# Head of a hybrid block: constants, loads and bias spread rearranged, rstd by GpSimd's power, batch 0's routing inside batch 1's scan

## Chip, cores and metric

The kernel runs on 1 core of one Trainium2 chip. The metric is device time in microseconds (us) of a run; less is better. Before the change it is 1699.86 us, the median of 6 runs (1697.03 to 1704.3).

## The reference

The input x is 8 batches of 512 tokens of 256 numbers, all float32. Four residual steps follow one another, each on a layernorm of x (written `_ln` here; mixture is `_L0_ffn_ref`, used twice with the same weights):

```python
x = x + scan(_ln(x))        # xi = silu(x @ Win + bin); h = 0.9*h + xi*Bp over time; y = h.Cp + Dp*xi; y @ Wout + bout
x = x + mixture(_ln(x))     # router, 4 of 16 experts (2 of 4 groups first), plus 2 shared experts
x = x + attention(_ln(x))   # 16 heads of 16, causal, scores clipped to +-10
x = x + mixture(_ln(x))
```

Since the decay is the same for all states, the scan of the 16 states of a channel is one scan of xi, times the sum over j of Bp * Cp. The bias bout is added to each token.

## The kernel before

A batch of 512 tokens is four tiles of 128 tokens (`NT`); features are taken in two halves (`KD`), the 512 scan channels in four columns of 128 (`NI`). There are four stages: the scan of all batches with the first mixture's routing and shared experts beside it (`stretch(Scan())`), the first mixture's routed blocks (`routed(0, ...)`), the attention with the second mixture's routing (`stretch(Attention())`), and the second mixture's routed blocks. The change lies in the first stage, which ends at about 370 us.

**Order.** Each engine runs its instructions in order; a planner chooses that order when the program is built, from the order in which the program issues them and from its own estimate of their times. `keep_in_program_order` pins an instruction, `issue_after` puts one behind another on the same engine. The program issues in pieces: `Piece` is a count of TensorE columns and a generator of steps; `behind` joins pieces one after another, `beside` interleaves them so that each has done the same share of its columns, and `timed` places the steps of a piece at given shares of what it is beside (0.2 is a fifth of the way). One pass of the loop at L1439 is called a slot here: slot b holds batch b's scan, batch b - 1's routing, batch b - 2's shared experts, and the norm and transposes of batch b + 1.

**Head.** `load_x(0)` brings batch 0's x (L147). GpSimd makes the identity (L173) and issues the DMAs of small weights (L180 to L197); bout goes through a DMA that spreads it over 128 partitions (L190). Then GpSimd makes the constants: `before` (L234), `causal` (L272), `tri` (L279), `ones` (L284), `region` by 16 memsets (L290), `steps`, `number`, `zeros` (L322). ACT issues the load of the scan's Win (L178) and Wout (L188).

**A norm** (`normed`, L436): VectorE takes statistics of each tile (L443, L444), and then rstd, the root's reciprocal, in one of two ways: by VectorE, three Newton steps after a start from the bits (L451 to L459), or by one addition on VectorE and a power on GpSimd (L462, L463). Then VectorE writes the normed tiles (L468). Batches 0 and 1 of the scan take the first way, and their instructions are pinned. `turned` (L393) transposes normed tiles on TensorE (L405) and copies them out of PSUM (L407).

**A scan** (`Scan.main`, L523) takes per column two matmuls into pz (L531), a sigmoid on ACT (L540), on VectorE the product (L541), the scan (L543) and, after ACT's scaling by Dp (L544), y (L547). Its steps are: four columns, one step of no work, then the projection by Wout (`add_projection`, 16 matmuls, L485), whose halves VectorE adds to x (L494). `Scan.project` (L514) adds bout to x on GpSimd (L518). Its `Piece` counts 10240 columns.

**Routing.** `Route` (L581): norm of the batch's x into `sorted_m`, transposes, the router's matmuls (`logits`, L622), then `choices` (L652): five steps of picking on VectorE (`PICKS`, L655 to L699), one with counting matmuls by tri and ones (L707, L708), two for slots and gains (the last instruction, L744, is kept in `gained`), and 16 steps, each with one indirect DMA from GpSimd (L758). In the scan stage the normed tiles of a batch are put behind the `gained` of the batch before (L603, L466). `shared_experts` (L1092) has 12 steps: eight of two wide matmuls (L1107), each pair of steps followed by ACT and VectorE (L1125 to L1127), and four of the down projection (L1136).

**The first two batches** (`first_two`, L1416): batch 0 is normed and turned before it. It issues load 2, batch 1's norm, the products of Bp and Cp (two entries of `pending`), batch 0's four columns, batch 1's transposes, bias sums and four columns, and batch 0's projection. What is left of batch 1's scan goes into slot 1, beside batch 0's routing with its picks, and batch 2's norm and transposes. Slot 2 begins the shared experts (batch 0's), and holds the rest of batch 0's choices.

Of the kernel before, what the change touches and what calls it, by code (L numbers as in the profile page):

```python
# [35 lines left out]
BLK = P  # L36
# [29 lines left out]
BY_PE = 3  # L66

# [15 lines left out]
def tile_hybrid_block(  # L83
# [87 lines left out]
    load_x(0)  # L171
    ident = const.tile([P, P], FP, name="ident")
    make_identity(nc, ident)  # L173

# [3 lines left out]
    nc.scalar.dma_start(out=w_in_sb, in_=w_in.rearrange("(p k) i -> p k i", p=P))  # L178
    b_in_sb = const.tile([P, NI], FP, name="b_in_sb")
# [14 lines left out]
    nc.gpsimd.memset(rw_sb, 0.0)  # L194
    nc.gpsimd.dma_start(out=rw_sb[:, :, 0:E], in_=router_t.rearrange("(p k) e -> p k e", p=P))
    rb_sb = const.tile([P, E], FP, name="rb_sb")
    nc.gpsimd.dma_start(out=rb_sb, in_=route_bias.partition_broadcast(P))  # L197
# [24 lines left out]
    def load_expert(e: int):  # L222
# [11 lines left out]
    nc.gpsimd.memset(before, 1.0)  # L234
    nc.gpsimd.affine_select(
        out=before,
        in_=before,
        compare_op=ALU.is_gt,
        fill=0.0,
        base=0,  # L240
        pattern=[[1, EG], [-1, EG]],
        channel_multiplier=0,
    )
    neg_half = const.tile([P, NT], FP, name="neg_half")
    nc.gpsimd.memset(neg_half, -0.5)
# [11 lines left out]
    def load_attention_weights():  # L257
# [14 lines left out]
    nc.gpsimd.memset(causal, TOP)  # L272
    nc.gpsimd.affine_select(
        out=causal, in_=causal, compare_op=ALU.is_ge, fill=0.0, base=0, pattern=[[0, 2], [1, P]], channel_multiplier=-1
    )
# [3 lines left out]
    nc.gpsimd.memset(tri, 1.0)  # L279
    nc.gpsimd.affine_select(  # L280
        out=tri, in_=tri, compare_op=ALU.is_gt, fill=0.0, base=0, pattern=[[1, P]], channel_multiplier=-1
    )
    ones = const.tile([P, P], FP, name="ones")
    nc.gpsimd.memset(ones, 1.0)  # L284
# [4 lines left out]
    for e in range(E):  # L289
        nc.gpsimd.memset(region[:, e : e + 1], float(e * REG))  # L290
    steps = const.tile([P, NJ], FP, name="steps")
    nc.gpsimd.iota(steps, [[BLK, NJ]], base=0, channel_multiplier=0, allow_small_or_imprecise_dtypes=True)
# [29 lines left out]
    nc.gpsimd.memset(zeros, 0.0)  # L322
    nc.gpsimd.iota(zeros[:, D + 2 * TK :].bitcast(I32), [[0, SAME]], base=NTOK, channel_multiplier=1)
# [62 lines left out]
    def issue(piece):  # L386
        for _ in piece.steps:
            pass


# [45 lines left out]
    def normed(b: int, tag: str, place, by_vector: bool = False, pinned: bool = False, past=lambda: None):  # L436
# [24 lines left out]
        else:  # L461
            nc.vector.tensor_scalar(rstd, mv[:, :, 1], EPS, None, ALU.add)  # L462
            nc.gpsimd.tensor_tensor(rstd, rstd, neg_half, ALU.pow)  # L463
# [911 lines left out]
    def stretch(layer):  # L1375
# [60 lines left out]
        begun = None  # L1436
        if layer.mixture == 0:
            begun = first_two()
        for b in range(1 if begun else 0, B):  # L1439
            pieces = [begun or layer.main(b, made.pop(b))]  # L1440
            begun = None
            nxt, last = b + layer.ahead, b == B - 1
            fill = []
            if layer.ahead > 1 and not last:
                fill.append(project(b + 1))
            if b > 1:
                shared_sum = experts(b - 2)
# [8 lines left out]
                pieces.append(timed(sends.pop(), 0.1, 0.14, 0.18, *spread(0.22, 0.66 if last else 0.86, NT * TK)))  # L1456
            if fill:
                pieces.append(behind(*fill))
            if b > 0:
# [3 lines left out]
                else:  # L1463
                    first, then, rows, full = layer.norms
# [8 lines left out]
                else:  # L1473
                    pieces += [
                        timed(r.scores(i == 1), *layer.scores[:2], *spread(*layer.scores[2:], NT)),
                        timed(some(r.rest, PICKS), *spread(*layer.choose, PICKS)),
                    ]
            if nxt < B:
                added = layer.load(nxt)
                if added is not None:  # L1480
# [3 lines left out]
                    timed(turn(nxt), *layer.turns),  # L1484
# [130 lines left out]
```

## Time and profile before

| | |
|---|---|
| median of 6 runs | 1699.86 us |
| the profiled execution: its own time | 1703.75 us |
| its span, first to last instruction | 1701.7 us |
| mean granted TensorE clock | 0.971 of full speed |
| busy, share of the span | PE 93%, PEld 68%, DVE 68%, ACT 44%, POOL 45% |
| batch 0's first normed tile (L468) starts | 8.50 us |
| batch 0's pz (L531) | from 11.62 us |
| batch 1's pz | from 29.10 us |
| batch 0's routing: first transposes (L405) | at 50.97 us |
| batch 2's pz, start of slot 2 | at 58.37 us |
| batch 3's pz, start of slot 3 | at 97.03 us |
| batch 4's pz, start of slot 4 | at 134.67 us |

PE is TensorE, PEld its weight loads (they overlap its matmuls), DVE VectorE, ACT ScalarE, POOL GpSimd; SP issues DMAs. A line of the timeline is: start, duration, engine, line, operation, output<-inputs, count, and in brackets the idle time before it with what ended it. A line of waits is: engine, tile and line that waited <- engine, tile and line that it waited for: us in total, times, longest. A float32 matmul appears as two records, so a step of two matmuls of 512 columns is four records.

### The profile page before, as it was taken

The page shows a single profiled execution, that of the slowest core. Times are in us where ns is not written, and L with a number is a line of the kernel's source. Part 1 is how long each engine was busy: PE and PEld are TensorE (multiplying, and loading weights), DVE is VectorE, ACT ScalarE, POOL GpSimd, SP SyncE. Part 2 cuts the span into 40 slices and gives each one's busy share as a digit, 9 for nine tenths or more (in the row PEclk, how much of TensorE's full clock was granted, in tenths as well). Part 3 has the DMA queues.
Part 4 walks back from the last instruction along what each step waited for, and adds up shares of the span by engine and source line. Part 5 has one row for each costly group of instructions (what it writes and reads, how often), then busy time and mean ns, then how long its engine had stood idle before and what let it go on. Part 6 is the DMA issues. An engine that isn't in the chain of part 4 may idle for free.

```text
span 1701.7 us, 34229 instructions
## 1 busy us (share of the span) xinstructions
PE 1585.1 (93%) x9992; PEld 1161.6 (68%) x9992; DVE 1155.6 (68%) x3623; ACT 743.9 (44%) x1461; POOL 758.6 (45%) x655
## 2 busy tenths in 40 slices
PE   6999995969999999999899999999896999999996
PEld 3566663559999999974344444454355999999996
DVE  7988885435677666647877876977753566666664
ACT  3223331125555555555553344353312555555553
POOL 3356654515555555540032422421451555555554
PEclk8999997989999999999999999999998999999998
DMA  4354421527777766641333224231652777777776
GB/s 163 135 197 152 147 97 63 187 61 109 102 126 123 104 99 98 92 73 38 87 95 107 90 88 125 78 104 67 196 182 63 109 102 127 135 135 135 133 135 131
DMA packets 281645, 195.31 MB, mean 115 GB/s; under 512 B 168592, under 2 KB 262064, under 8 KB 281456
## 3 DMA queue, kind: packets, MB, share of 16 engines
q1 hardware_dynamic: 228368, 119.40, 27.5%
q0 software_dynamic: 51984, 72.09, 23.8%
q8 instruction: 85, 1.39, 0.3%
q10 hardware_dynamic: 1104, 1.57, 0.3%
q14 instruction: 104, 0.85, 0.2%
HBM read 89.71 MB, written 103.23 MB: 113 GB/s over the span
## 4 chain that ended last, share of the span: by engine, by line
PE 34%; DVE 10%; DMA 4%; issue 2%; another core or an unknown queue 1%; ACT 1%; POOL 0%; SPq 0%; DVEq 0%; POOLq 0%; ACTq 0%
PE ph L993 13%; PE pyr L1024 6%; PE pd_m L1136 3%; PE pg_m L1107 3%; DMA part<-rows 3%; PE ps_a L1238 2%; PE po_a L1274 2%; DVE w_all L1258 2%; DVE w_all L1259 1%; DMA x<-part 1%; PE py_a L485 1%; PE pv_a L1208 1%; PE pq_a L1190 1%; PE pt L975 1%
## 5 line engine op out<-in xcount | busy, mean ns | idle before, releaser
L1034 POOL DMA_INDIRECT part<-rows x272 | 426.3, 1567 | 340.1 <-ACT rows L1033 252.4
L758 POOL DMA_INDIRECT xg<-sorted_m,slots_m x256 | 259.8, 1015 | 272.9 <-ACT slots_m L755 94.5
L993 PEld LDWEIGHTS ph<-rows,gate 128*128 128x128 f32 x2160 | 277.8, 191 | 33.4 <-ACT rows L976 22.2
L993 PE MATMUL ph<-rows,gate 128*128 128x128 f32 x2160 | 291.5, 278 | 1.9 <-ACT rows L976 1.9
L993 PE MATMUL ph<-rows,up 128*128 128x128 f32 x2160 | 285.3, 275 | 0.0
L1024 PE MATMUL pyr<-w_all,rows 128*128 x1088 | 279.2, 380 | 0.0
L993 PEld LDWEIGHTS ph<-rows,up 128*128 128x128 f32 x2160 | 262.9, 192 | 0.0
L966 DVE COPY up<-w_all 128x512 f32 x270 | 119.1, 442 | 211.4 <-PE ph L993 192.5
L966 ACT COPY gate<-w_all 128x512 f32 x270 | 166.5, 618 | 122.5 <-DVE up L966 55.3
L1024 PEld LDWEIGHTS pyr<-w_all,rows 128*128 128x128 f32 x1088 | 186.9, 192 | 14.3
L1248 ACT ACTIVATE w_all<-ps_a 128x1024 f32<-128x1024 f32 x160 | 155.4, 1021 | 75.7 <-PE ps_a L1238 49.9
L1033 ACT ACTIVATE rows<-pyr,gain 128x256 f32<-128x256 f32 x272 | 128.9, 474 | 80.9 <-PE pyr L1024 60.6
L1001 ACT ACTIVATE rows<-ph 128x256 f32<-128x256 f32 x272 | 104.5, 384 | 114.2 <-PE ph L993 103.0
L1003 DVE TENSOR_TENSOR rows<-ph,rows 128x256 f32<-128x256 f32 x272 | 115.1, 423 | 32.1 <-ACT rows L1001 30.7
L1004 DVE TENSOR_TENSOR rows<-ph,rows 128x256 f32<-128x256 f32 x272 | 115.3, 424 | 26.2 <-issue 0.5
L1136 PE MATMUL pd_m<-sd_sb,act_m 128*128 128x256 f32 x512 | 121.2, 382 | 5.9 <-DVE sig_m L1122 5.7
L1107 PE MATMUL pg_m<-xT_m,su_sb 128*128 128x512 f32 x256 | 125.4, 611 | 0.6 <-issue 0.6
L1107 PE MATMUL pg_m<-xT_m,sg_sb 128*128 128x512 f32 x256 | 123.9, 607 | 0.0
L1238 PE MATMUL ps_a<-w_all 32*128 32x384 f32 (+3 forms) x1024 | 111.4, 478 | 10.9 <-ACT w_all L1248 10.2
L1136 PEld LDWEIGHTS pd_m<-sd_sb,act_m 128*128 128x128 f32 x512 | 95.8, 190 | 27.5 <-DVE sig_m L1122 7.6
L1258 DVE SCALAR_TENSOR_TENSOR w_all<-w_all,causal 128x512 f32<-128x512 f32 (+1 forms) x160 | 92.4, 578 | 28.8 <-ACT w_all L1248 25.5
L1238 PEld LDWEIGHTS ps_a<-w_all 32*128 32x128 f32 x1024 | 48.6, 189 | 72.3 <-ACT w_all L1248 44.7
(213 smaller groups left out, 1960.6 us busy)
## 6 DMA issues: line engine op xcount, KB each, us to landing
rows<-xg SPq DMA_DIRECT2D x720, 32.0 KB
rows<-xg SPq DMA_DIRECT2D x92, 134.0 KB
part<-x SPq DMA_DIRECT2D x16, 512.0 KB
part<-ys_m SPq DMA_DIRECT2D x14, 512.0 KB
sum<-part SPq DMA_DIRECT2D x14, 512.0 KB
w_all<-in_L_ffn_gate_w_dram SPq DMA_DIRECT2D x27, 256.0 KB
w_all<-in_L_ffn_up_w_dram SPq DMA_DIRECT2D x27, 256.0 KB
w_all<-in_L_ffn_down_w_dram SPq DMA_DIRECT2D x27, 256.0 KB
```

Of the source, the lines that this page charges most:

```text
L758: nc.gpsimd.indirect_dma_start(out=xg[i], out_offset=bass.IndirectOffsetOnAxis(ap=slots[:, at : at + 1], axis=0), in_=rows[:, t, :], in_of ...
L966: copy(here, w_all[:, bass.ds(held[n][0] + half * KD * F, KD * F)])
L993: nc.tensor.matmul(ph[s][:, f * P : (f + 1) * P], lhsT=both[s][:, k * F + f * P : k * F + (f + 1) * P], rhs=rows[:, ROW + k * P : ROW + (k ...
L1004: made = nc.vector.tensor_mul(act, ph[1], act)
L1024: nc.tensor.matmul(py, lhsT=act[:, f * P : (f + 1) * P], rhs=w_all[:, bass.ds(w + 2 * KD * F + f * D, D)], start=(f == 0), stop=(f == KF - 1),
L1033: nc.scalar.mul(y, py, gain[:, TK : TK + 1])
L1034: acc = nc.gpsimd.indirect_dma_start(out=parts[i][n % 2], out_offset=bass.IndirectOffsetOnAxis(ap=rows[:, D + 2 * TK : D + 2 * TK + 1].bit ...
L1107: made = nc.tensor.matmul(dst, lhsT=w[:, k, f * P : (f + 1) * P], rhs=xnT[:, k, :], start=(k == 0), stop=(k == KD - 1),)
L1136: nc.tensor.matmul(py[:, j, :], lhsT=acts[n][:, f, t * P : (t + 1) * P], rhs=shared[n][3][:, f, :], start=(n == 0 and f == 0), stop=(n == ...
L1238: nc.tensor.matmul(ps[j // 2][:, j % 2, col : col + n], lhsT=k_sb[w][r, o, c * P : (c + 1) * P], rhs=q_sb[r, o, c * P : T], start=True, st ...
L1248: nc.scalar.activation(es[two], ps[two], AF.Exp, scale=ATT_SCALE)
L1258: nc.vector.scalar_tensor_tensor(diagonal, diagonal, LOW, limit, ALU.max, ALU.min)
```

## The change

It does the following.

- `ones` and `neg_half` are made first, by VectorE; `steps` is dropped; `region` is one iota. `zeros`, the router's loads, `before`, `causal` and `tri` go into a list `late`, which is issued behind the power of batch 1's norm.
- bout is loaded as one row and spread over the partitions by a matmul with a row of ones and a copy on ACT. Wout's load goes from ACT's queue to SP's, behind x 1.
- 14 matmuls of ones by ones (`keep_busy`) stand at TensorE's start, 5 more after batch 0's projection.
- rstd of batches 0 and 1 comes by GpSimd's power; both copies of batch 0's transposes go to ACT.
- In `first_two` the order is: batch 0's bias sums, batch 1's statistics and power, the two products, batch 1's normed tiles, the shared weights' loads, the late constants, load 2; then two columns of batch 0, batch 1's transposes, two columns of batch 0, two of batch 1, batch 0's projection. Two columns of batch 1 and its bias sums are left to slot 1.
- In slot 1 batch 0's routing begins at once (places 0.0 to 0.1), four of the twelve shared-expert steps of batch 0 stand at 0.35 to 0.8, batch 2's transposes at 0.93. The five picks of batch 0 move from slot 1 to the start of slot 2 (0.02 to 0.2), which keeps eight of the expert steps; batch 1's scores and picks move to later places in slot 2.

The diff, cut:

```diff
+IDLE, FIRST, BETWEEN, EARLY = 14, 2, 5, 4
...
     load_x(0)
+    ones = const.tile([P, P], FP, name="ones")
+    nc.vector.memset(ones, 1.0)
+    neg_half = const.tile([P, NT], FP, name="neg_half")
+    nc.vector.memset(neg_half, -0.5)
...
+    b_out_sb = const.tile([P, D], FP, name="b_out_sb")
+    nc.gpsimd.dma_start(out=b_out_sb[0:1, :], in_=b_out.rearrange("(o d) -> o d", o=1))
...
-    nc.scalar.dma_start(out=w_out_sb, in_=w_out.rearrange("(c p) d -> p c d", p=P))
-    b_out_sb = const.tile([P, D], FP, name="b_out_sb")
-    nc.gpsimd.dma_start(out=b_out_sb, in_=b_out.partition_broadcast(P))
     load_x(1)
+    nc.sync.dma_start(out=w_out_sb, in_=w_out.rearrange("(c p) d -> p c d", p=P))
...
-    for e in range(E):
-        nc.gpsimd.memset(region[:, e : e + 1], float(e * REG))
-    steps = const.tile([P, NJ], FP, name="steps")
-    nc.gpsimd.iota(steps, [[BLK, NJ]], base=0, channel_multiplier=0, allow_small_or_imprecise_dtypes=True)
+    nc.gpsimd.iota(region, [[REG, E]], base=0, channel_multiplier=0, allow_small_or_imprecise_dtypes=True)
...
+    def keep_busy(many: int, name: str):
+
+        idle = bank([P, P], f"idle_{name}")
+        for _ in range(many):
+            nc.tensor.matmul(idle, lhsT=ones, rhs=ones, start=True, stop=True)
...
-            nc.vector.tensor_scalar(rstd, mv[:, :, 1], EPS, None, ALU.add)
-            nc.gpsimd.tensor_tensor(rstd, rstd, neg_half, ALU.pow)
+            keep(nc.vector.tensor_scalar(rstd, mv[:, :, 1], EPS, None, ALU.add))
+            powers[tag] = nc.gpsimd.tensor_tensor(rstd, rstd, neg_half, ALU.pow)
+            if pinned:
+                yield
...
-            return normed(b, f"l{i}_{b}", place, first, first)
+            return normed(b, f"l{i}_{b}", place, False, first)
...
+        if i == 0:
+            keep_busy(IDLE, "head")
+            spread_row = bank([P, D], "b_out")
+            nc.tensor.matmul(spread_row, lhsT=ones[0:1, :], rhs=b_out_sb[0:1, :], start=True, stop=True)
+            nc.scalar.copy(b_out_sb, spread_row)
...
-                issue(Piece(0, turn(b, by_both if first else layer.copies)))
-                if first:
-                    load_shared()
-            if b == 0:
+                issue(Piece(0, turn(b)))
+            if b == 0 and i == 1:
                 issue(project(b))
 
         def first_two():
 
-            layer.load(1)
-            issue(Piece(0, norm(1, True)))
+            issue(project(0))
+            second = norm(1, True)
+            issue(Piece(0, some(second, NT + 1)))
             for _ in range(2):
                 pending.pop(0)()
+            issue(Piece(0, second))
+            load_shared()
+            with tc.issue_after(powers["l0_1"].ins):
+                for make in late:
+                    make()
+            layer.load(1)
             main = layer.main(0, made.pop(0))
-            issue(Piece(0, some(main.steps, NI)))
+            issue(Piece(0, some(main.steps, FIRST)))
             issue(Piece(0, turn(1)))
-            issue(project(1))
+            issue(Piece(0, some(main.steps, NI - FIRST)))
+            later_sum = project(1)
             second = layer.main(1, made.pop(1))
-            issue(Piece(0, some(second.steps, NI)))
+            issue(Piece(0, some(second.steps, NI - 2)))
             issue(main)
-            return Piece(second.columns - NI * KD * T, second.steps)
+            keep_busy(BETWEEN, "between")
+            return behind(Piece(second.columns - (NI - 2) * KD * T, second.steps)), later_sum
...
+            scores, choose, turns = layer.scores, layer.choose, layer.turns
+            if i == 0 and b == 1:
+
+                scores, turns = (0.2, 0.22, 0.5, 0.55), (0.93, 0.95)
+            if i == 0 and b == 2:
+                scores, choose = (0.61, 0.65, 0.73, 0.77), (0.79, 0.99)
...
+            if i == 0 and b == 1:
+                piece = experts(0)
+                each = piece.columns // 12
+                started[0] = Piece((12 - EARLY) * each, piece.steps)
+                pieces.append(timed(some(piece.steps, EARLY), *spread(0.35, 0.8, EARLY)))
+                pieces.append(timed(later_sum.steps, *spread(0.12, 0.3, NT)))
             if b > 1:
-                shared_sum = experts(b - 2)
+                shared_sum = started.pop(b - 2, None) or experts(b - 2)
...
+                if i == 0 and b == 2:
+                    pieces.append(timed(sends.pop(), *spread(0.02, 0.2, PICKS), 0.22, 0.24, 0.26, *spread(0.32, 0.88, NT * TK)))
...
-                    first, then, rows, full = layer.norms
+                    first, then, rows, full = layer.norms if i or b > 1 else (0.0, 0.04, 0.06, 0.1)
...
-                        timed(r.scores(i == 1), *layer.scores[:2], *spread(*layer.scores[2:], NT)),
-                        timed(some(r.rest, PICKS), *spread(*layer.choose, PICKS)),
+                        timed(r.scores(i == 1), *scores[:2], *spread(*scores[2:], NT)),
+                        *([timed(some(r.rest, PICKS), *spread(*choose, PICKS))] if i or b > 1 else []),
```

More of the change, by code (lines that the diff above doesn't have):

```diff
@@ L171, in tile_hybrid_block @@
     load_x(0)
+    ones = const.tile([P, P], FP, name="ones")
+    nc.vector.memset(ones, 1.0)
+    neg_half = const.tile([P, NT], FP, name="neg_half")
+    nc.vector.memset(neg_half, -0.5)
     ident = const.tile([P, P], FP, name="ident")
     make_identity(nc, ident)
+    late, powers = [], {}
     w_scan = const.tile([P, 2 * KD * DI], FP, tag="w_sa", name="w_scan")
@@ L187, in tile_hybrid_block, with load_router @@
     w_out_sb = w_scan[:, KD * DI :].rearrange("p (c d) -> p c d", c=NI)
-    nc.scalar.dma_start(out=w_out_sb, in_=w_out.rearrange("(c p) d -> p c d", p=P))
-    b_out_sb = const.tile([P, D], FP, name="b_out_sb")
-    nc.gpsimd.dma_start(out=b_out_sb, in_=b_out.partition_broadcast(P))
     load_x(1)
+    nc.sync.dma_start(out=w_out_sb, in_=w_out.rearrange("(c p) d -> p c d", p=P))
     rw_sb = const.tile([P, KD, SQ], FP, name="rw_sb")
-    nc.gpsimd.memset(rw_sb, 0.0)
-    nc.gpsimd.dma_start(out=rw_sb[:, :, 0:E], in_=router_t.rearrange("(p k) e -> p k e", p=P))
     rb_sb = const.tile([P, E], FP, name="rb_sb")
-    nc.gpsimd.dma_start(out=rb_sb, in_=route_bias.partition_broadcast(P))
+    def load_router():
+        nc.gpsimd.memset(rw_sb, 0.0)
+        nc.gpsimd.dma_start(out=rw_sb[:, :, 0:E], in_=router_t.rearrange("(p k) e -> p k e", p=P))
+        nc.gpsimd.dma_start(out=rb_sb, in_=route_bias.partition_broadcast(P))
+    late.append(load_router)
     pending = []
@@ L233, in tile_hybrid_block, with make_before @@
     before = const.tile([P, EG, EG], FP, name="before")
[L234 to L245, printed above, removed]
+    def make_before():
+        nc.gpsimd.memset(before, 1.0)
+        nc.gpsimd.affine_select(
+            out=before,
+            in_=before,
+            compare_op=ALU.is_gt,
+            fill=0.0,
+            base=0,
+            pattern=[[1, EG], [-1, EG]],
+            channel_multiplier=0,
+        )
+    late.append(make_before)
     decay = const.tile([P, 1], FP, name="decay")
@@ L271, in tile_hybrid_block, with make_causal, make_tri @@
     causal = const.tile([P, 2, P], FP, name="causal")
[L272 to L275, printed above, removed]
-    tri = const.tile([P, P], FP, name="tri")
[L279 to L284, printed above, removed]
+    def make_causal():
+        nc.gpsimd.memset(causal, TOP)
+        nc.gpsimd.affine_select(
+            out=causal, in_=causal, compare_op=ALU.is_ge, fill=0.0, base=0, pattern=[[0, 2], [1, P]], channel_multiplier=-1
+        )
+    late.append(make_causal)
+    tri = const.tile([P, P], FP, name="tri")
+    def make_tri():
+        nc.gpsimd.memset(tri, 1.0)
+        nc.gpsimd.affine_select(
+            out=tri, in_=tri, compare_op=ALU.is_gt, fill=0.0, base=0, pattern=[[1, P]], channel_multiplier=-1
+        )
+    late.append(make_tri)
     numbers = const.tile([P, E], FP, name="numbers")
@@ L321, in tile_hybrid_block, with make_zeros @@
     zeros = const.tile([P, ROW], FP, name="zeros")
-    nc.gpsimd.memset(zeros, 0.0)
-    nc.gpsimd.iota(zeros[:, D + 2 * TK :].bitcast(I32), [[0, SAME]], base=NTOK, channel_multiplier=1)
+    def make_zeros():
+        nc.gpsimd.memset(zeros, 0.0)
+        nc.gpsimd.iota(zeros[:, D + 2 * TK :].bitcast(I32), [[0, SAME]], base=NTOK, channel_multiplier=1)
+    late.insert(0, make_zeros)
     later = [lambda e=e: load_expert(e) for e in range(E)]
@@ L1434, in start_route @@
             return routes[b]
-        begun = None
+        begun, started = None, {}
         if layer.mixture == 0:
-            begun = first_two()
+            begun, later_sum = first_two()
         for b in range(1 if begun else 0, B):
@@ L1455, in stretch @@
                 fill.append(shared_sum)
-                pieces.append(timed(sends.pop(), 0.1, 0.14, 0.18, *spread(0.22, 0.66 if last else 0.86, NT * TK)))
+                if i == 0 and b == 2:
+                    pieces.append(timed(sends.pop(), *spread(0.02, 0.2, PICKS), 0.22, 0.24, 0.26, *spread(0.32, 0.88, NT * TK)))
+                else:
+                    pieces.append(
+                        timed(sends.pop(), 0.1, 0.14, 0.18, *spread(0.22, 0.66 if last else 0.86, NT * TK))
+                    )
             if fill:
@@ L1483, in stretch @@
                     timed(norm(nxt), *spread(0.32, 0.44, NT), *spread(0.56, 0.64, NT)),
-                    timed(turn(nxt), *layer.turns),
+                    timed(turn(nxt), *turns),
                 ]
```

## The prediction, made before the result

> **What bounds the kernel now.** I read the page's slices first (40 equal slices, 42.5 us each, busy tenths and granted clock).
>
> ```profile
> PE   6999995969999999999899999999896999999996
> DVE  7988885435677666647877876977753566666664
> PEclk8999997989999999999999999999998999999998
> ```
>
> TensorE is nearly full everywhere except in the first slice, in slices 7 and 9 (the passage from the scan to the routed blocks) and in a few later seams. The change works in slice 1 and on the border to slice 2, so I next read the head in stretches cut where TensorE starts and stops. Columns: PE, PEld, DVE, ACT, POOL busy us (instructions), then the clock, DMA share, GB/s.
>
> ```profile
> 0.00:9.20 9.20, 0.00 (x0) 0.00 (x1) 5.28 (x23) 1.49 (x2) 8.09 (x41) 1.00 0.69 209
> 9.20:22.46 13.26, 9.97 (x24) 4.77 (x25) 11.45 (x32) 3.98 (x6) 3.30 (x7) 1.00 1.04 363
> 22.46:29.10 6.64, 2.34 (x9) 1.26 (x9) 6.42 (x10) 1.94 (x4) 2.98 (x4) 0.54 0.08 27
> 29.10:33.40 4.30, 4.30 (x5) 1.84 (x6) 2.14 (x3) 1.64 (x3) 0.00 (x0) 0.51 0.00 0
> 33.40:48.65 15.25, 15.25 (x60) 11.02 (x58) 14.41 (x28) 5.04 (x8) 0.00 (x0) 1.00 0.00 1
> 48.65:50.97 2.32, 0.00 (x1) 0.04 (x1) 1.19 (x7) 0.00 (x0) 1.65 (x3) 1.00 0.68 230
> 50.97:58.37 7.40, 7.15 (x49) 5.59 (x50) 7.33 (x30) 2.40 (x5) 3.54 (x5) 1.00 0.69 241
> ```
>
> Of 58.4 us TensorE is busy 39.0, and 4.3 of those run at half clock. VectorE is busy 48: it sets the head. The waits of TensorE alone in these 58.4 us say where the rest goes:
>
> ```profile
> PE pt_l L405 <- POOL region L290: 9.2, 1, 9.2
> PE pz_s L531 <- ACT xT_l L407: 4.1, 1, 4.1
> PE pt_l L405 <- DVE xn L468: 3.1, 1, 3.1
> PE pt_m L405 <- DVE sorted_m L468: 2.3, 1, 2.3
> ```
>
> The first is put down to the memsets of region, but xn ends its first tile at 8.98, so VectorE's chain is as late. After that comes the steady part (same columns):
>
> ```profile
> 57.00:97.03 40.03, 39.57 (x157) 25.27 (x155) 35.59 (x125) 11.51 (x27) 19.14 (x21) 1.00 0.50 178
> 97.03:134.67 37.64, 37.64 (x149) 24.00 (x148) 33.15 (x117) 11.99 (x27) 21.33 (x24) 1.00 0.48 167
> ```
>
> From 51 us until 262 TensorE has no gap: one slot (one batch's scan with an earlier batch's experts beside it) takes 37.6 us. So work taken out of a slot shortens it, as long as VectorE (33.2 of 37.6) keeps up, and the whole change is worth what TensorE idles less before 58.4.
>
> **The change, step by step.** Durations from the profiled execution (span 1701.7, time 1703.75, 3.9 above the median 1699.86); the difference is then taken from the median.
>
> ```profile
> 5.65 0.17 DVE L451 TENSOR_SCALAR var_l<-mv_l 128x4 f32<-128x4 f32 x1
> ...
> 8.50 1.90 DVE L468 TENSOR_SCALAR xn<-x,mv_l,rstd_l 128x256 f32<-128x256 f32 x4
> ...
> 49.32 1.05 POOL L463 TENSOR_TENSOR rstd_m<-rstd_m,neg_half 128x4 f32<-128x4 f32 x1 [23.86 <-DVE rstd_l L462]
> ...
> 50.41 1.38 DVE L468 TENSOR_SCALAR sorted_m<-x,mv_m,rstd_m 128x256 f32<-128x256 f32 x4 [1.09 <-POOL rstd_m L463]
> ```
>
> *rstd by power.* Today VectorE needs from 5.65 to 8.50, 2.85 us, for batch 0's rstd. The power row exists: rstd_m's first step at 49.07, power 49.32 to 50.37, next tile at 50.41, so 1.34 us. Queued before it on GpSimd are five DMA issues (today four and the identity end at 5.02, the new first one 0.55: 5.57) and three iotas (0.14, 0.14, 0.26): free at about 6.1, not 5.82. Then xn starts at 7.2 instead of 8.5: 1.3 gained. For batch 1 the power's wait is covered by the two bc operations (24.12 to 25.16, 1.04).
>
> The Trainium skill, "GPSIMD Engine Reference", section Engine selection, speaks against this: elementwise work belongs on VectorE, GpSimd being about twice as slow with two inputs. By that rule, as an estimate, the power step would take twice 2.85, so xn 4.4 later than I put it, and the gain below would be about 6. The row of 1.05 us decides: it replaces eleven dependent operations, not one.
>
> *First projections.* The transposes follow at 7.9 (today 9.23), pz at about 10.2 (11.62). Both PSUM copies now go to ACT, 0.59 each; VectorE loses the 0.69 at 11.84.
>
> *VectorE to the first route.* xn ends at 9.1; stats of batch 1 as for batch 0 (3.39 to 5.62) 2.2: 11.3; power and bc 1.3: 12.6; xn (21.99 to 24.12) 2.1: 14.7. A scan column costs 2.67 (scan starts at 37.10, 39.78, 42.45). Batch 0's four: 25.4 (today 32.03); batch 1's first two: 30.7; the two sums 1.35, the route's stats 2.0: 34.1; power 1.34: 35.4; a scan in progress may add 0.3, and the first sorted tile lets the transposes start at 36.1, not 50.97.
>
> *TensorE meanwhile.* pz columns at 1.72 each: batch 0's and two of batch 1's with the transposes end near 22.9. The projection of batch 0 (16 matmuls, 0.43 each) waits for y at 25.4 and ends at 31.0; five idle matmuls 1.1; batch 1's last two columns to 35.5. From 38.1 (36.1 plus today's 1.98 from the first transposes to the use of xT) it is full: four expert steps 6.86, logits 0.65, projection 1 (its y, 34.1 + 1.4 + 5.3 = 40.9, is in time) 6.86, transposes 0.95: slot 1 ends at 53.5. Today it ends at 58.37, with 6.86 of expert work still to do: 58.37 + 6.86 - 53.5 = **11.7 us**. TensorE's own ceiling: 39.8 us of work from 7.9 on ends at 47.7, a gain of 17.5.
>
> *Slot 2.* It loses the four steps on TensorE: 37.6 - 6.9 = 30.8. VectorE loses two pairs of L1126 and L1127 (2.7 summed, 2.5 as busy time, since operations overlap by 8%) and gains batch 0's choices (6.3 summed by their rows, 5.8): 33.2 + 5.8 - 2.5 = 36.5. So VectorE falls up to 5.7 behind. The places leave some 6 us between a tile's VectorE step and TensorE's use of it (y at 0.3 to 0.4 of the slot, projection from 0.6; sorted at 0.4, turned at 0.61), and slot 3 gives 4.4 back. I charge 1 us, between 0 and 5.7. Sum: **10.7 gained**.
>
> *Costed at nothing.* The spread of the bias: the one-row matmul and its copy are not in the trace; a matmul there takes 0.25 to 1.2 us and the ACT copy at most 0.59; TensorE and ACT are idle until 7.9. Its DMA landed at most 8.5 us after its issue (5.01, used at 13.55); issued now at 1.40, it is there between 2 and 10, and the transposes queue behind it on TensorE: 0 to 2 us of loss; I take 0, since the x rows, issued at 0.81, are in use at 3.39. Fourteen idle matmuls: 28 records, 3 us at 0.107 and 6 at half clock, over before 7.9 either way. Five idle ones: covered while VectorE works until 34.1; 1.1 otherwise. The late constants, 3.5 us of GpSimd behind batch 1's power, and w_out, shared weights, x 2 and the experts behind x 1 on SP: GpSimd's own bias sums (3.0) are due at 27, w_out at 23, the shared weights at 38; the 1.5 MB take 4 us at 380 GB/s. Cover over 10 us; without it each us counts once.
>
> *Clock.* A gap of 3.1 us at 19.3 was followed by half clock, one of 2.3 at 48.65 was not. The new gap, 22.9 to 25.4, is 2.5: I take no loss; half clock for 3.9 us, as today, would cost 1.9.
>
> The Trainium skill, "TensorE: Matmul & The Clock Gate", Part 1, says that the array starts throttled and needs about 3.4 us of activity. Here the clock stands at 1.00 before any matmul and the first batch's pz take 0.43 to 0.48 a record. By the rule the fourteen idle matmuls would bring up to 1.7 us more; by the row nothing, and I go by the row.
>
> **Rivals.**
>
> *VectorE binds slot 2.* For it: 36.5 against 30.8, and the waits it has in every slot (4.4 of 37.6). Then slot 2 ends when VectorE has begun it at 50.5 and worked 36.5 plus 4: at 91 instead of 97.03, a gain of 6: 1694. Against: the spare places above.
>
> *The route is no earlier.* The whole gain is the time by which batch 0's sorted tiles come before 50.4. If the order on VectorE puts all of batch 1's scan columns, and waits between them as at 31.3 to 34.4 today, ahead of the route, its tiles come at about 45, TensorE idles 9 us after 35.5, then half clock 1.9: slot 1 ends at 64, gain 1 or so: 1699. For it: a planner orders the engines' work, and today it let VectorE idle 4 us there. Against: the route's places are 0 to 0.1.
>
> *Slower.* One mechanism: the tail. At 273 to 289 TensorE waits 15.6 us for the choices of batch 6 (L707 for sel_m), while those of batch 7 at 319.9 cost none. The planner orders the tail by its own estimate of times; if the shifted start turns that order so that batch 7's counts also end the wait, 15.6 come on top: 1689 + 15.6 = 1704.8. It decides from 14 us of new waiting on. Against: the diff touches no place after slot 2.
>
> **How the numbers follow.** Forecast (gain 8 to 17) 0.60, **1689**; VectorE binds (gain 3.5 to 8) 0.21; route no earlier (within 3.4) 0.12; tail 0.07. About 0.2%, 3.4 us, is what a measurement here can tell from no change. Faster 0.81, same 0.12, slower 0.07. The range goes from the ceiling of 17.5 (1682) to a gain of 2 (1698): 11.7 less VectorE's 5.7, 2 for a late bias and 1.9 for half clock. Outside lie most of the third case and the tail. Against the profiled execution the forecast reads 1693.
>
> **What would show it.** xn of batch 0 at 7.2 and the power before it (1.3 step); y of batch 0 done near 25; the first route's transposes near 36; slot 1's end (batch 2's first pz) near 53.5; batch 3's first pz near 85 with TensorE unbroken between; the clock at 1.00 from 10 to 60. The forecast is wrong if the sorted tiles come after 42, if TensorE shows gaps beyond 3 us in slots 2 and 3, or if the tail from 262 on, shifted by 11, takes longer than today's.

## The result, and the profile after

The changed kernel takes 1707.74 us (median of 23 runs, 1702.21 to 1715.68) against 1701.2 for the kernel before (49 runs, 1692.51 to 1706.08): ratio 1.0043, 95% interval 1.0032 to 1.0053 (the quotient of these two medians is 1.0038). It is slower by 6.5 us where 10.7 less were forecast. The profiled execution took 1710.31 us with a span of 1708.6; that of the kernel before took 1703.75. Line numbers of the changed kernel are higher by 25 in the transposes and the norm's statistics (L407 is now L432, L443 is L468, the power is L488), and by 27 from the normed tiles on (L468 is now L495, L531 is L558).

The slices of the changed kernel's page:

```profile
PE   8889995979999999999899999999896999999996
DVE  7778885536667766647877967877753666666664
PEclk9999998989999999999999999999998999999998
```

TensorE's first digit is 8 instead of 6, as the head's new order would have it; the second and third are 8 and 8 instead of 9 and 9. A slice is 43 us, too coarse for what follows. Slots are read from the first pz of each batch (us):

| kernel | slot 1 ends | slot 2 lasts | slot 3 lasts | batch 4's pz |
|---|---|---|---|---|
| before | 58.37 | 38.66 | 37.64 | 134.67 |
| forecast | 53.5 | 31.8 | - | - |
| changed | 61.28 | 44.18 | 39.13 | 144.59 |

From batch 4 to the last scan slot both kernels run at 37.5 a slot. Busy times of the changed kernel between its landmarks (from:to, length, then PE, PEld, DVE, ACT, POOL busy, the granted clock, DMA share, GB/s):

```profile
0.00:7.22 7.22, 6.10 (x30) 5.86 (x30) 2.53 (x13) 1.49 (x2) 5.96 (x15) 1.00 0.59 166
10.26:22.05 11.79, 10.40 (x24) 5.08 (x25) 9.76 (x21) 4.49 (x8) 9.07 (x17) 0.86 1.06 354
22.05:39.52 17.47, 15.32 (x59) 9.96 (x58) 15.74 (x35) 5.92 (x10) 2.28 (x5) 1.00 0.18 64
39.52:61.28 21.76, 19.28 (x80) 12.34 (x80) 17.04 (x42) 4.92 (x10) 3.62 (x5) 0.92 0.41 139
61.28:105.46 44.18, 34.50 (x133) 21.81 (x133) 30.80 (x110) 10.11 (x24) 19.65 (x21) 0.92 0.37 125
105.46:144.59 39.13, 39.13 (x149) 24.66 (x150) 34.42 (x120) 12.29 (x29) 21.34 (x23) 0.96 0.46 158
```

The fifth row holds most of the loss. Slot 2 has less TensorE work than before, and still lasts 5.5 us longer; TensorE is idle for 9.7 us of it, VectorE for 13.4. Neither engine is full: they wait for each other, or for something else. What TensorE waited for from 22 to 146 us:

```profile
PE pr_m L734 <- DVE sel_m L726: 4.3, 1, 4.3
PE py_s L512 <- issue: 3.6, 5, 1.0
PE py_s L512 <- DVE y_s L574: 2.7, 2, 1.8
PE pg_m L1134 <- ACT xT_m L432: 2.3, 1, 2.3
```

The first two lines are the subject of the experiments. Where the first stands in TensorE's order:

```profile
68.25 1.88 PE L558 MATMUL pz_s<-xT_l,w_scan 128*128 128x512 f32 x4
74.41 0.66 PE L734 MATMUL pr_m<-sel_m,tri 128*128 128x64 f32 x2 [4.28 <-DVE sel_m L726]
...
75.29 3.19 PE L1134 MATMUL pg_m<-xT_m,sg_sb 128*128 128x512 f32 x4
78.31 1.88 PE L558 MATMUL pz_s<-xT_l,w_scan 128*128 128x512 f32 x4
```

The matmuls that count batch 0's choices (L734, L735; place 0.22 of the slot) come after three pz columns and before the fourth. They wait 4.28 us for VectorE's sel_m; behind them stand expert steps and the last pz column, which VectorE's scan needs. The four records after the wait take 3.19 us instead of 1.88; the granted clock is 0.70 on average from 74.4 to 80.0 us. (Below, "half clock" stands for stretches in which the granted clock falls like this; from 102 to 104 us it is 0.50.)

The second line is stranger. From 98 to 104 us TensorE and VectorE both start an instruction only about every 0.7 us (or a multiple), with nothing recorded that most of them wait for:

```profile
100.44 0.38 PE L512 MATMUL py_s<-w_scan,y_s 128*128 128x256 f32 x1 [1.03 <-issue]
101.18 0.38 PE L512 MATMUL py_s<-w_scan,y_s 128*128 128x256 f32 x1 [0.36 <-issue]
102.59 0.78 PE L512 MATMUL py_s<-w_scan,y_s 128*128 128x256 f32 x1 [1.03 <-issue]
```

```profile
99.07 0.18 DVE L469 BATCH_NORM_AGGREGATE mv_l<-stats_l 128x2 f32<-128x6 f32 x1 [0.47 <-DVE eq_gm L598]
99.76 0.23 DVE L599 TENSOR_TENSOR gt_gm<-gt_gm,eq_gm 128x64 f32<-128x64 f32 x1 [0.51 <-issue]
101.18 0.22 DVE L600 TENSOR_REDUCE sel_gm<-gt_gm 128x16 f32<-128x64 f32 x1 [1.20 <-DVE gt_gm L599]
```

### The profile page after: what moved, and what is told of

It reads as the page before. It is cut to its first block, busy times and chain, and to the rows that moved or that the text cites. A ratio compares the mean times of both kernels' runs of the same rounds, so it can differ in the third digit from the quotient of the medians.

```text
span 1708.6 us, 34271 instructions
## 1 busy us (share of the span) xinstructions
PE 1597.2 (93%) x10032; PEld 1170.2 (68%) x10032; DVE 1151.4 (67%) x3602; ACT 743.7 (44%) x1463; POOL 761.8 (45%) x639
## 4 chain that ended last, share of the span: by engine, by line
PE 36%; DVE 9%; DMA 3%; issue 1%; ACT 1%; another core or an unknown queue 1%; SPq 0%; POOL 0%; DVEq 0%; POOLq 0%; ACTq 0%
PE ph L1020 13%; PE pyr L1051 6%; PE pg_m L1134 4%; PE pd_m L1163 3%; PE ps_a L1265 3%; PE po_a L1301 2%; DMA part<-rows 2%; DVE w_all L1285 2%; PE py_a L512 1%; PE pv_a L1235 1%; DVE w_all L1286 1%; PE pq_a L1217 1%; DMA x<-part 1%; ACT w_all L1275 1%
```

## The experiments

They ran on several chips, and the chips differ: on two the kernel before takes 1698 to 1700 us, much as in the result above (called A), on three 1643 to 1645 (called B). Most of B's lead lies outside the changed stretch (the rebuilt head alone, profiled on both, is 1.1 us ahead at batch 4 on B, and 26.6 where the routed blocks begin, at 335.84 against 362.48 us). So a ratio is always to the kernel before on the same chip, and slots are compared within a kind. Each chip was used for one group of runs only, so A and B may be a state of the chip as well as its kind; the kernel before was profiled on A alone.

Three parts of the change can be undone one by one: the rebuilt head (constants, loads, bias, power, the order of slots 0 and 1), the four early expert steps, and the move of batch 0's choices into slot 2.

### Parts undone, on a chip of kind A

Choices back in slot 1, their counts and sends at the places of before:

```
-  *([timed(some(r.rest, PICKS), *spread(*choose, PICKS))] if i or b > 1 else []),
+  timed(some(r.rest, PICKS), *spread(*choose, PICKS)),
-  if i == 0 and b == 2:
-      pieces.append(timed(sends.pop(), *spread(0.02, 0.2, PICKS), 0.22, ...
```

> The changed kernel with one part undone: batch 0's five picks stand in slot 1 again (places 0.71 to 0.97), and its counts and sends in slot 2 at the places of before. Theory A (the picks, moved in front of slot 2, keep TensorE waiting at the counting matmuls: 4.3 us idle at 70.1 and 1.5 of half clock after it): slot 2 (batch 2's pz to batch 3's) shrinks from 44.2 to about 38, the time falls by about 6 from the changed kernel's 1708 to about 1702. Theory B (the stall from 98.3 to 104, where TensorE and VectorE start an instruction only every 0.7 us while DMAs run full, is the main loss and has nothing to do with the picks): the wait at the counts goes, the stall stays, and the time is about 1704 to 1708. Theory C (the four early expert steps are what disturbs VectorE): no change, 1707 to 1709.

No early expert steps:

```
-IDLE, FIRST, BETWEEN, EARLY = 14, 2, 5, 4
+IDLE, FIRST, BETWEEN, EARLY = 14, 2, 5, 0
```

> The changed kernel with EARLY = 0: all twelve expert steps of batch 0 in slot 2, the picks still in slot 2. Theory A: slot 2 now has 37.6 us of TensorE work, the counts come later in TensorE's order by two or three steps but the picks still stand before them: wait at the counts 1 to 4 us, slot 1 ends at about 54, slot 2 at about 95 to 98, time about 1700 to 1703. Theory B: as before the change within 2 us, 1700 to 1706, with the stall somewhere in slot 2. Theory C: about 1697 or less, slot 2 without gaps.

Both edits, that is, the rebuilt head alone:

> Both undone: picks in slot 1, no early steps; what is left is the rebuilt head with its order of the first two batches. Theory A: no wait at the counts; slot 1 ends at about 55 instead of 58.4, slot 2 takes 37.6 to 39: gain of 2 to 4 over the kernel before, about 1697 to 1699. Theory B: the stall may remain (plus 6): 1703. Theory C: the same as A here, 1697.

The changed kernel with the counts and sends later:

```
-  0.22, 0.24, 0.26, *spread(0.32, 0.88, NT * TK)
+  0.46, 0.5, 0.54, *spread(0.58, 0.98, NT * TK)
```

> The changed kernel with only batch 0's counts, slots, gains and sends moved later in slot 2 (0.46, 0.5, 0.54, then 0.58 to 0.98, instead of 0.22 to 0.88); the picks stay in slot 2. Theory A: TensorE finds the picks done, the wait of 4.3 and its half clock go: about 1702, slot 2 about 38. Theory B: the sends move past the expert loads, so less of both at once; if the stall comes from both it goes too: about 1696 to 1700; if not, 1703. Theory C: 1707 to 1709.

| on A (before 1699.91) | us | ratio, interval | slot 1 ends | slot 2 | slot 3 |
|---|---|---|---|---|---|
| choices back in slot 1 | 1702.6 | 1.0011 (0.9998 to 1.0024) | 60.85 | 33.31 | 44.45 |
| no early steps | 1699.08 | 0.999 (0.9974 to 1.0005) | 51.72 | 40.16 | 42.67 |
| head alone | 1692.88 | 0.9966 (0.995 to 0.9982) | 52.00 | 37.63 | 39.61 |
| counts later | 1712.78 | 1.007 (1.0045 to 1.0094) | 59.19 | 35.26 | 54.32 |

The head alone wins 7.0 us. Each of the other two parts, added to it, takes that away: the early steps 9.7 us (1702.6 - 1692.88), the moved choices 6.2. Later counts remove the wait at the counting matmuls, and slot 3 then loses more than slot 2 wins: VectorE starts nothing from 94.74 to 109.10 us there, although the projection that its next instruction reads ends at 94.6. The other variants have such late starts too (below, "Chip or program"), so on A the price of a part is not told apart from them.

### Work left out, rstd, idle matmuls, copies, on a chip of kind B

Four expert steps of batch 0 left out, on the head alone:

```
-            for n in range(NSH):
+            skipped = 1 if i == 0 and b == 0 else 0
+            for n in range(skipped, NSH):
...
+            acts = acts * 2 if skipped else acts
```

> The rebuilt head alone, and in slot 2 the four expert steps that the change would have done early are left out altogether (gate and up of the first shared expert for batch 0's tokens; both halves of the down projection read the second expert's result): TensorE has 6.86 us less in slot 2, VectorE two pairs of products less, and slot 1 is untouched by early steps. Theory A (in slots 2 and 3 TensorE and VectorE wait for each other in their fixed orders, so TensorE's work can be taken out of slot 2 without the end of slot 3 coming earlier): slot 2 near 33, slot 3 near 44, their sum 75 to 77 against 77.2 of the rebuilt head alone, time 1691 to 1693. Theory B (the saving is kept, and the change loses it only by what the early steps do to slot 1): slots 2 and 3 together 70.3, time 1686.

The head alone with VectorE's rstd (`normed(..., first, first)` again):

> The rebuilt head alone, with rstd of batches 0 and 1 by VectorE's eleven operations again. Theory of the recorded step (the power gives xn of batch 0 1.3 us earlier and all that follows with it): 1.3 later for batch 0 and up to 1.3 more for batch 1, so 1694.2 to 1695.5 against 1692.9. Rival (VectorE waits 2.15 us for batch 1's rows in the head anyway, and slot 1 ends on other things): no difference beyond 0.5, 1692.4 to 1693.4, with batch 2's first pz at 52.

The head alone with `IDLE, BETWEEN = 0, 0`:

> The rebuilt head alone, without the fourteen idle matmuls in front and the five between. Recorded step (the clock stands at 1.00 before any matmul, so they give nothing): same time within 0.7, 1692.2 to 1693.6, first pz matmuls at 0.43 a record. Rival (they keep the clock up): first pz at half clock, up to 1.7 us later in the head, and about 1.9 more at the first wait behind batch 1's projection: 1694.5 to 1696.5.

The changed kernel with `Route(i, b, by_both if i == 0 and b == 0 else layer.copies)`:

> The changed kernel, with batch 0's routed tiles copied out of PSUM by ACT and VectorE in turn instead of ACT alone. Theory A (slot 1's lateness is not what sets the end; slots 2 and 3 lose whatever is won before them): slot 1 ends 1 to 4 earlier than 61.3, slots 2 and 3 together longer by as much, time within 2.5 of 1707.7. Theory D (the ACT copies that queue behind the scan's multiplication make slot 1 late, and the half clock that follows the wait is part of it): the wait of 2.28 in front of the first expert matmuls and the 1.96 of half clock go, slot 1 ends at 57, time 1703.5. Rival: the copies on VectorE come behind scan columns, and slot 1 ends later than 61.3, up to 2 us.

| on B (before 1643.26) | us | ratio, interval | slot 1 ends | slot 2 | slot 3 |
|---|---|---|---|---|---|
| four steps left out | 1635.71 | 0.9946 (0.9929 to 0.9964) | 51.81 | 36.55 | 38.39 |
| rstd on VectorE | 1638.33 | 0.9969 (0.9956 to 0.9983) | 54.84 | 37.63 | 37.71 |
| no idle matmuls | 1639.41 | 0.9968 (0.9949 to 0.9986) | 53.02 | 37.64 | 37.70 |
| copies shared | 1643.5 | 1.0002 (0.999 to 1.0013) | 59.65 | 38.14 | 38.01 |

Leaving 6.86 us of TensorE's work out of slot 2 altogether brings next to nothing: slots 2 and 3 take 74.9 us, and 75.4 with that work (the head alone on another chip of kind B, next section). VectorE is a large part of why. In that run, from 44 to 72 us and from 72 to 80:

```profile
44.00:72.00 28.00, 25.10 (x98) 14.93 (x92) 27.57 (x91) 8.98 (x19) 8.78 (x10) 1.00 0.29 101
72.00:80.00 8.00, 7.48 (x35) 6.07 (x38) 2.77 (x8) 1.36 (x4) 6.17 (x7) 0.79 0.74 246
```

VectorE works 27.57 of 28 us; then it is TensorE's turn, and VectorE idles. A mean over the slot (30.9 of 36.6) shows neither. How large that part is, the next section's relief of VectorE shows.

The power is worth 2 to 3 us at slot 1's end (54.84 against 51.81 to 52.80 in the three runs on B that leave slots 0 and 1 of the head alone as they are). Sharing the copies does not remove the wait before the first expert step (2.29 us): the first of the two copies still runs on ACT behind its multiplication of the scan. So this run does not decide theory D; slot 1 ends at 59.65, and the time is no better.

### The changed kernel again, and VectorE relieved, on another chip of kind B

The first two are unchanged files. In the other two the product of gate and sigmoid is left out for batches 0 and 1:

```
-                        nc.vector.tensor_mul(sig, ph, sig)
+                        if b > 1:
+                            nc.vector.tensor_mul(sig, ph, sig)
```

> The changed kernel itself once more, beside its own variants on one chip. If the stretch in which TensorE and VectorE start an instruction only every 0.7 us (98 to 104 us in the changed kernel's profile) belongs to the program (Theory B): it comes again near 98 to 104, and batch 3's first pz near 105. If it is an event of single executions: no such stretch, batch 3's first pz near 98 to 100, and the time against the kernel before still 3 to 7 us longer in the median of many runs, since slots 2 and 3 lose without it (Theory A).

> The rebuilt head alone once more, beside the changed kernel and its variants on one chip: 7.0 us under the kernel before as at the first time (by 4 to 9), batch 2's first pz at 52, slots 2 and 3 together 77.

> The rebuilt head alone with the four expert steps of slot 2 left out, as before, and with VectorE's product of gate and sigmoid left out too in batch 0's and batch 1's experts (the sigmoid takes the gate's place): VectorE loses two instructions of 0.68 us in slot 2 and four in slot 3, 4.1 us in all; TensorE's work is that of the run with four steps left out. Theory A (VectorE's work sets how soon slots 2 and 3 end): 3 to 4 us less than that run, slots 2 and 3 together 71 to 72. Theory O (only the fixed order and its places set it, not VectorE's amount of work): within 1 us of that run, slots 2 and 3 together 74 to 75.

> The changed kernel with VectorE's product of gate and sigmoid left out in batch 0's and batch 1's experts (the sigmoid takes the gate's place): VectorE loses two instructions of 0.68 us in slot 1, two in slot 2 and four in slot 3, 5.4 us in all. Theory A (VectorE's work sets how soon slots 1 to 3 end): 4 to 5.5 us less than the changed kernel on the same chip. Theory O (the places in the order set it): less than 1.5 us less, the wait at the counting matmuls still above 3.

| on B (before 1644.39) | us | ratio, interval | slot 1 ends | slot 2 | slot 3 |
|---|---|---|---|---|---|
| changed kernel | 1642.5 | 0.9991 (0.998 to 1.0003) | 60.40 | 38.15 | 38.04 |
| head alone | 1635.62 | 0.9944 (0.9923 to 0.9966) | 52.77 | 37.65 | 37.72 |
| four steps out, relieved | 1635.44 | 0.9943 (0.9923 to 0.9963) | 52.80 | 35.85 | 37.52 |
| changed, relieved | 1643.56 | 0.9992 (0.9977 to 1.0006) | 60.79 | 37.60 | 37.52 |

Two things follow. Taking 5.4 us off VectorE in the changed kernel brings nothing: its amount of work is not what holds that kernel, and theory A in this form fell. (With the four steps left out, relief of 4.1 us shortens slots 2 and 3 by 1.6, to 73.4, between the 71 to 72 and the 74 to 75 of the two theories, and the time by nothing: 1635.44 against 1635.71.) And on B the changed kernel has no stretch of late starts; slot 2 is 38.15, not 44.18. Its wait at the counts (4.27), the half clock behind it and the wait for y (0.92) are there all the same:

```profile
73.52 0.41 PE L734 MATMUL pr_m<-sel_m,tri 128*128 128x64 f32 x2 [4.27 <-DVE sel_m L726]
73.77 0.39 PE L735 MATMUL pr_m<-sel_m,ones 128*128 128x64 f32 x2
73.99 3.08 PE L1134 MATMUL pg_m<-xT_m,sg_sb 128*128 128x512 f32 x4
76.86 2.48 PE L558 MATMUL pz_s<-xT_l,w_scan 128*128 128x512 f32 x4
```

### Order against amount, on a third chip of kind B

> The changed kernel with batch 0's choices back in slot 1, once more, beside its relieved form. As at the first time: slot 2 near 33, slot 3 near 44, where TensorE waits for batch 1's sorted tiles, VectorE busy nearly without a break before slot 3's first projection matmul. Time against the kernel before: plus 3 at the first chip; near 0 where the clock holds.

> The changed kernel with batch 0's choices back in slot 1 and VectorE's product of gate and sigmoid left out in batch 0's and batch 1's experts (the sigmoid takes the gate's place): 5.4 us less VectorE work in slots 1 to 3. Theory A' (with the counts out of the way, VectorE's backlog sets the end of slot 3): 3.5 to 5.4 us less than the same kernel unrelieved on the same chip, slot 3 near 40. Theory O (order and places alone): within 1 us.

> The changed kernel with batch 0's counts and sends later in slot 2, once more. Theory A' (counts only move the wait; VectorE's backlog is paid in slot 3): the wait of 4.3 at the counting matmuls is gone, slot 2 near 35, slot 3 41 to 44, slots 2 and 3 together 76 to 79, no less than the changed kernel's 76.2. Theory O (the counts ahead of the fourth pz column are the whole loss): slots 2 and 3 together 71 to 72 and a time 4 us less than the changed kernel. If the stretch of one instruction every 0.7 us comes again near 102 to 108, it belongs to this program, whatever the chip.

> The changed kernel without the early expert steps (choices still in slot 2), once more, beside the form with the choices back in slot 1. Theory (each of the two parts costs the rebuilt head what it had won, mostly in slots 2 and 3): within 3 us of the form with choices back in slot 1, both 5 to 9 us above the rebuilt head alone, that is, 1 to 3 us on either side of the kernel before.

| on B (before 1645.33) | us | ratio, interval | slot 1 ends | slot 2 | slot 3 |
|---|---|---|---|---|---|
| choices back in slot 1 | 1638.86 | 0.9961 (0.9948 to 0.9974) | 59.93 | 32.49 | 38.78 |
| the same, relieved | 1638.72 | 0.9956 (0.9942 to 0.997) | 60.95 | 32.48 | 37.51 |
| counts later | 1640.58 | 0.9966 (0.9953 to 0.9978) | 60.15 | 35.38 | 37.51 |
| no early steps | 1638.71 | 0.9958 (0.9945 to 0.9971) | 52.24 | 41.32 | 37.92 |

With the choices in slot 1 the counting matmuls find their input ready, and slot 2 is 32.49, near the 31.8 of the forecast. Slot 2 of that run:

```profile
63.47 1.88 PE L558 MATMUL pz_s<-xT_l,w_scan 128*128 128x512 f32 x4
65.19 0.33 PE L734 MATMUL pr_m<-sel_m,tri 128*128 128x64 f32 x2
```

```profile
59.93:92.42 32.49, 31.48 (x132) 21.15 (x133) 28.04 (x91) 11.26 (x26) 16.03 (x18) 1.00 0.43 153
```

No bracket stands behind the counting matmul, so it waits for nothing, and TensorE is busy 31.48 of 32.49 us, against 32.95 of 38.15 in the changed kernel on B. Counts moved later give 3.3 of the 4.9 us that slots 2 and 3 together differ by (76.2 changed, 72.9 counts later, 71.3 choices in slot 1); 72.9 lies in neither forecast, nearer to theory O's 71 to 72 than to the 76 to 79 of its rival. So on B it is the order that costs these 5 us (theory O), and not VectorE's amount of work: relief of VectorE gives under 1 us of time (0.9956 against 0.9961). On A this is not shown: there the later counts cost time.

### Chip or program

> The kernel before, unchanged, traced on the same chip as the changed kernel. Theory A' (the change's early steps and moved choices take from slots 2 and 3 what they win before): batch 2's first pz at 58.4 and batch 4's at 134 to 135, as in its first profile, so that the changed kernel, at 136 on chips without the stall, has lost all of its head's gain by slot 3's end. If it is a chip's difference: batch 4's first pz of this kernel at 140 or later.

> The changed kernel itself, beside the kernel before on one chip. On a chip where the kernel before takes 1640 to 1650: ratio 0.998 to 1.001, no stretch of one instruction every 0.7 us. On a chip where it takes 1700: ratio 1.003 to 1.006 and the stretch near 98 to 104 again. A stretch on a chip of the first kind, or its absence on one of the second with the same ratio, speaks against the stall as the cause of the difference between chips.

These two ran on a second chip of kind A. The kernel before: 1698.36 us (ratio to its own other runs 0.9991, 0.9978 to 1.0003), batch 4's pz at 134.31. The changed kernel: 1706.83, ratio 1.0046 (1.0032 to 1.006), slots 2 and 3 of 44.16 and 39.34 us, the late starts at 98 to 104 us again. The stretch stands in both profiles of this program on A and not in the one on B. On A late starts fall on other variants too. The choices-in-slot-1 kernel, one file, after the last matmul of the logits, first on A, then on B:

```profile
85.46:90.55 5.09, 5.09 (x28) 4.62 (x28) 0.16 (x1) 0.00 (x0) 4.29 (x6) 1.00 1.01 370
```

```profile
84.50:89.60 5.10, 5.10 (x31) 4.63 (x28) 5.10 (x23) 1.41 (x4) 4.31 (x5) 1.00 1.03 372
```

TensorE, GpSimd and the DMA do the same on both; VectorE works 0.16 us on A and 5.10 on B, ACT nothing on A. VectorE's next instruction on A is

```profile
90.55 0.32 DVE L667 STREAM_TRANSPOSE logit_m<-pl_m 128x128 f32<-128x128 f32 x1 [4.93 <-remote]
```

though its input was ready at 85.46. On all A profiles but one this transpose in slot 2 is late: by 1.1 us in the kernel before, 3.0 in the head alone, 3.3 in the changed kernel, 4.7 without early steps and 5.1 here; with later counts the 14.4 us of idle VectorE come instead. On B the variants and the changed kernel have it 0.1 us after its input. Slot 3 of this kernel is 44.45 on A and 38.78 on B; with later counts it is 54.32 and 37.51. What holds the engines there is not settled: the DMA is as full on B (1.03), and no run varied the loads or the sends alone on A.

The best version found is the rebuilt head alone: 0.9966 on A and 0.9944 on B, ahead of both kernels on both kinds.

## Why the prediction was wrong

**Head: right in order, a little late.** xn of batch 0 starts at 7.22 (7.2 forecast) behind the power, pz at 10.26 (10.2).

```profile
6.14 1.05 POOL L488 TENSOR_TENSOR rstd_l<-rstd_l,neg_half 128x4 f32<-128x4 f32 x1
7.22 1.79 DVE L495 TENSOR_SCALAR xn<-x,mv_l,rstd_l 128x256 f32<-128x256 f32 x4 [1.15 <-POOL rstd_l L488]
...
11.16 0.43 DVE L468 BATCH_NORM_STATS2 stats_l<-x 128x6 f32<-128x256 f32 x1 [2.15 <-DMA x<-in_L_attn_a_x_dram]
```

The third row is what was missed: batch 1's rows land at 11.16, VectorE waits 2.15 us, TensorE's next transposes come after a gap, and the pz behind them start at half clock (granted clock 0.59 from 16 to 18 us and 0.56 from 18 to 20; 0.86 over the second row of the stages), where the forecast had 1.00 from 10 to 60. y of batch 0 is done at 28.7 (25.4 forecast), the route's first transposes are at 39.52 (36.1).

**Slot 1: the size failed.** The step "slot 1 ends at 53.5" gave 61.28: 7.8 us. Of these 3.4 are the late route, 2.1 the longer way from the route's transposes to the first expert step (4.1 us against 1.98 assumed: ACT's copies stand behind its multiplication of the scan, L571, which waits for VectorE), and 1.8 half clock after that wait (3.68 us for four records, 1.88 at full clock), which the other profiles of this kernel do not show; 0.5 is left over. Against the head alone on B the four steps, 6.86 us of work, lengthen slot 1 by 7.2 to 7.6.

```profile
42.39 0.72 ACT L571 ACTIVATE xi_s<-xi_s,d_sb 128x512 f32<-128x512 f32 x1 [2.43 <-DVE state_s L570]
```

```profile
43.63 3.68 PE L1134 MATMUL pg_m<-xT_m,sg_sb 128*128 128x512 f32 x4 [2.28 <-ACT xT_m L432]
```

**Slot 2: this is the step that failed.** "The places leave some 6 us between a tile's VectorE step and TensorE's use of it ... I charge 1 us, between 0 and 5.7." Slot 2 took 44.18 instead of 31.8. The charge was 13.4 on A (44.18 - 30.8) and 7.4 on B. The spare places were read for y and the sorted tiles; the one place the change itself had set, the counts at 0.22 behind choices spread to 0.2, was not read. In the profile on B VectorE has sel_m, behind two scan columns, a pair of expert products and all of the picks, at 73.4 us; TensorE is at the counts at 69.3 (73.52 - 4.27).

```profile
72.80 0.58 DVE L726 TENSOR_REDUCE sel_m<-pick_m 128x64 f32<-128x256 f32 x1
```

On B this makes up 7.0 of the 7.4: 4.3 of wait, 1.8 of half clock (3.08 and 2.48 us for groups of 1.88), 0.9 for y. On A slot 2 is 6.0 us longer still, about the length of the stretch of late starts, whose cause is open; slot 3 begins with 1.6 at half clock behind it (batch 3's first four records take 3.48). At batch 4 the changed kernel is 21.7 us behind the forecast (122.9, with 37.6 for slot 3): 7.8 from slot 1, 6.4 from slot 2 as on B, 6.0 from slot 2 on A alone, 1.5 from slot 3.

A slip in the sum decides nothing: the 30.8 starts from 37.6, which is slot 3's length, while slot 2 of the kernel before took 38.66. So the forecast gain of 10.7 goes with batch 3's pz at 86.3, not near 85. Two readings are a little off as well: TensorE has gaps of 0.25 and 0.46 us between 51 and 262 us, and the 2.34 us of TensorE in the third row of the first table of stretches ran at a granted clock of 0.54 too, beside the 4.3.

**What the early steps are worth.** With the choices in slot 1, on B, they cost slot 1 7.2 us and slots 2 and 3 give 4.1 back (71.3 against 75.4): a net loss of 3.1 at batch 4, within the noise of the ratios (0.9961 against 0.9944). The forecast took both sides as 6.86. On A nothing comes back (77.8 against 77.2), but there 5.1 us of late start stand in slot 2 of the one and 3.0 in that of the other.

**The rivals.** None foresaw it. "VectorE binds slot 2" had the right slot and the wrong cause: VectorE's work in slot 2 was 30.8 us, not 36.5, and relief of VectorE changes no time. "The route is no earlier" is refuted (39.52 against 50.97), "slower" did not come by the tail: the changed kernel is 9.9 us behind at batch 4 and 6.9 at the end. The prediction's own sign of being wrong, a gap beyond 3 us on TensorE in slot 2, did come.

**The clock at the start: read wrongly.** The prediction took the clock column's 1.00 for full speed before any matmul. Without the fourteen idle matmuls the first pz records are longer:

```profile
10.49 5.66 PE L558 MATMUL pz_s<-xT_l,w_scan 128*128 128x512 f32 x8
```

Eight records take 5.66 us; with the idle matmuls, on B:

```profile
10.13 3.70 PE L558 MATMUL pz_s<-xT_l,w_scan 128*128 128x512 f32 x8 [0.32 <-ACT xT_l L432]
```

In the changed kernel the fourteen idle matmuls themselves take 5.76 us for 28 records; the five later ones take 1.28 for 10:

```profile
1.12 5.76 PE L414 MATMUL idle_head<-ones 128*128 128x128 f32 x28 [1.12 <-DVE decay L259]
```

So TensorE starts slow, and 2 us of pz are the price of leaving the idle matmuls out. The Trainium skill's rule in "TensorE: Matmul & The Clock Gate", Part 1 (throttled at the start, released by activity) agrees with these rows. The clock column has no record that early: the first stands at 14.5 us without the idle matmuls and at 6.4 in the run with them on B, and before it the column reads 1.00. Yet slot 1 ends at 53.02, only 0.2 to 1.2 us later than in the runs on B with them (51.81 to 52.80); that VectorE's scan is what is late there is argued, not tested.

## What to carry to other kernels

Work taken off the bound engine in one stage is won only as far as each instruction in that engine's order finds its input there: for every wait that a move creates or brings nearer, compare when the input is made with when the engine arrives, and look at what queues behind it (here one pz column, and with it the other engine's scan). Work moved earlier costs where it goes as surely as it frees where it was; test the parts of a compound change singly, for here one part had all the gain. And measure on more than one chip: the same file was 0.45% slower on one kind and even on the other.

## What the runs showed of the hardware

- Two kinds of chips: 1698 to 1700 and 1643 to 1645 us for one kernel. On the slower kind VectorE at times starts nothing for 5 us (14 in one variant), or VectorE and TensorE one instruction per 0.7 us. Loads and the sends of the choices fill the DMA when this begins (share 1.01 in the first case, 1.10 from 98 to 100 us in the second), but not until it ends (0.23 from 102 to 104); the cause is open.
- VectorE's small two-input instructions can last as long as one of GpSimd's sums. On A, three of a kind that takes 0.17 us elsewhere took 0.73 to 0.76; the second and third ran beside two sums of 0.7, the first began 0.6 us ahead of their recorded start:

```profile
92.22 0.73 DVE L691 TENSOR_TENSOR top_m<-hi_m 128x16 f32<-128x16 f32 x1
92.87 0.76 DVE L692 TENSOR_TENSOR top_m<-hi_m 128x16 f32<-128x16 f32 x1
93.54 0.74 DVE L693 TENSOR_TENSOR top_m<-lo_m 128x16 f32<-128x16 f32 x1
```

```profile
92.83 1.41 POOL L545 TENSOR_TENSOR x<-x,b_out_sb 128x256 f32<-128x256 f32 x2
```

The Trainium skill, "SBUF — State Buffer", section Who interferes with whom, says that a VectorE instruction with two inputs in SBUF contends with a GpSimd instruction that reads SBUF; the second and third row agree.
